# Layer 3 of a four-layer graph network: softmax per block instead of per chunk, and block ends placed by columns

## The chip, the cores and the metric

The kernel runs on one core of a Trainium2 chip. A core has TensorE (PE, matrix products), VectorE (DVE, elementwise work and reductions), ScalarE (ACT, functions such as Exp and Tanh), GpSimd (POOL) and SyncE (SP); every engine works through its own queue in order. Transfers are carried out by 16 DMA engines; a transfer with an index per row ("indirect") is issued from POOL. The metric is the device time of one launch in microseconds, as the median of several runs.

## The reference

3125 nodes with 256 features, 53125 edges sorted by their target. Four layers follow each other; each normalizes x, computes something over the edges and adds it to x. Only layer 3 is changed, a graph attention followed by one gated step:

```
xp = h @ W.T;  a_src = xp @ att_src;  a_dst = xp @ att_dst
src, dst = edges and one loop from each node to itself
e = leaky_relu(a_src[src] + a_dst[dst], 0.2)
alpha = softmax of e over the edges of each target
agg = sum over the edges of a target of alpha * xp[src]
hb = tanh(agg + bias);  i, g, o = hb @ W_ih.T, split (f is not needed)
x = x + sigmoid(o) * tanh(sigmoid(i) * tanh(g))
```

## The kernel before

The nodes are sorted by their number of edges and cut into 25 blocks of 128, one node in each partition. Block b has SLOTS[b] columns: 36 for the first, 24 for the second, and down to 9 for the last, 439 in all. Column q holds the q-th edge of each of the block's nodes, or an empty slot that a penalty `pen` keeps out of the softmax. Before layer 3's edges begin, a table of rows is written to DRAM, one row of 514 numbers for each node: xp (256), a_src, a_dst, and x itself (256).

For each block, one indirect gather ("own", line 1252 by way of line 154) fetches the nodes' own rows, and one gather for every column fetches the first 258 numbers of the source rows into `xg` (also line 154). So there are 439 gathers of columns and 25 of own rows on POOL.

The columns of a block are handled in chunks of at most eight, 66 chunks in all. After a chunk's gathers, VectorE forms the scores z (line 1312), applies the leaky slope (1314) and the penalty (1315), takes the chunk's maximum (1317) and the running maximum (1318), and the difference to the old one (1320). ScalarE takes Exp of the difference (1321) and of the scores (1325). VectorE then sums the denominator (1328, 1330 or 1332), rescales the weighted sum so far (1335), and adds every column times its weight (1338). That is a running softmax. The node's own loop is the start of the sum: its score is the first maximum (1295, 1298), and the own row is the first sum.

The end of a block, `ended`, is a generator in four parts: division and bias and Tanh (1258 to 1262); two transposes and the products with W_ih in four matmuls (1268, 1270); Sigmoid, Tanh and the products (1273 to 1279); and the scatter of the finished rows to the output (line 158). One part is taken per chunk, after that chunk's gathers are written down: so the four parts of a block's end are spread over the first four chunks that follow it.

Three things set the order of the work. Gathers and scatters keep the order in which the program writes them, by explicit links (`queued`, line 139): a gather stands behind every earlier gather and scatter, a scatter behind the last gather. On the other engines a planner lays the instructions in the queue: it prefers what the program writes first, but fills gaps with later work that it takes to be ready. And buffers: `xg` has 6 tiles of 8 columns, `own` 4 tiles, `z3`, `sc3` and `ex` two each.

Of the kernel before, what the change touches and what calls it, by code (L numbers as in the profile page):

```python
# [9 lines left out]
F32 = mybir.dt.float32  # L10
I32 = mybir.dt.int32
BF = mybir.dt.bfloat16
AF = mybir.ActivationFunctionType
ALU = mybir.AluOpType
AX = mybir.AxisListType
# [3 lines left out]
P = 128  # L19
N = 3125  # L20
NB = 25
NP = NB * P
# [3 lines left out]
D = 256  # L26
# [15 lines left out]
SLOTS = (36, 24, 23, 22, 21, 20, 20, 19, 19, 18, 18, 17, 17, 17, 16, 16, 15, 15, 14, 14, 13, 13, 12, 11, 9)  # L42
HALF = tuple((s + 1) // 2 for s in SLOTS)
SM = 36
# [9 lines left out]
XPR = 514  # L54


def flat(ap, n):

    return bass.AP(tensor=ap.tensor, offset=ap.offset, ap=[[n, 1], [1, n]])
# [104 lines left out]
def rows(b):  # L164
    return LAST if b == NB - 1 else P
# [338 lines left out]
def by_slots(ctx, tc, a, out, a_d, nodes_d, ss, t):  # L504
    nc = tc.nc

    def dram(name, shape):
        return nc.dram_tensor(name, shape, F32, kind="Internal").ap()
# [7 lines left out]
    xp_d = dram("s_l3_rows", [NP, XPR])  # L516

    const = ctx.enter_context(tc.tile_pool(name="s_const", bufs=1))
    k = Kit(tc, const)
    Kit.last[:] = [None, None]  # L520
    ident, pcol, jrow = k.ident, k.pcol, k.jrow
    nid_i, nid3_i, deg, has, src_t, pen = t.nid_i, t.nid3_i, t.deg, t.has, t.st[:, :, :, 0], t.pen
# [38 lines left out]
    with tc.tile_pool(name="s_e0", bufs=2) as wk, tc.tile_pool(name="s_e0w", bufs=1) as w, \  # L561
# [42 lines left out]
        for to, of in ((bq, wq), (bkv, wkv)):  # L604
            m = of.shape[2]
            pm = ps.tile([P, 512], F32, name="pm")
            for q in range(2):
                nc.tensor.matmul(pm[:, 0:m], qc[:, q:q + 1].to_broadcast([P, P]), of[:, q, :],
                                 start=(q == 0), stop=(q == 1))
# [129 lines left out]
        def step(n):  # L739

            for _ in range(n):
                if work and next(work[0], work) is work:
                    work.pop(0)
            for t in list(late):
                t[0] -= 1
                if t[0] <= 0:
                    late.remove(t)
                    t[1]()
# [22 lines left out]
        for b in range(NB):  # L771
            S = HALF[b]
            at_, m = ahead
            acc = wk.tile([P, 2, 512], F32, name="acc")
            for s in range(S):
                messages(b, s, stat, m, acc)
                if s == 1 and before is not None:
                    end(b - 1, before)
                if s == S // 2 and b + 1 < NB:
                    ahead = begin(b + 1)  # L780
                if s % 4 == 3 and s + 1 < S:
                    stat = turned(b, at_, s + 1)
                elif s + 1 == S and b + 1 < NB:
                    stat = turned(b + 1, ahead[0], 0)
                if b:
                    scatter_src(1)
                step(1)
            before = acc
        end(NB - 1, before)
        while work or late:  # L790
            step(1)
# [14 lines left out]
    with tc.tile_pool(name="s_e1", bufs=2) as wk, tc.tile_pool(name="s_e1w", bufs=1) as w, \  # L806
# [142 lines left out]
        soon, calm, late1 = [], [], []  # L949
# [14 lines left out]
        for b in range(NB):  # L964
# [4 lines left out]
            sc = wk.tile([P, SM, 4], F32, name="sc")  # L969
            kvs = []  # L970
            for s0 in range(0, SLOTS[b], U):
                s1 = min(s0 + U, SLOTS[b])
# [20 lines left out]
    src3 = apool.tile([P, NB, SM], I32, name="src3")  # L993
    nc.vector.tensor_scalar(src3, src_t, float(XPR), None, op0=ALU.mult)

    wit = apool.tile([P, 2, 768], F32, name="wit")
# [5 lines left out]
    with tc.tile_pool(name="s_e2", bufs=2) as wk, tc.tile_pool(name="s_e2w", bufs=1) as w, \  # L1002
# [8 lines left out]
        for o, (of, cc) in enumerate([("L3_gnn_W_ih", c) for c in (0, 1, 6, 7, 4, 5)] + [("L3_gnn_W", c) for c in (0, 1)]):  # L1011
# [5 lines left out]
            to = wit[:, :, o * P:(o + 1) * P] if o < 6 else wt[:, :, (o - 6) * P:(o - 5) * P]  # L1017
            nc.scalar.copy(to, pt[:, 0:2, :])
        for i, of in enumerate(("L3_gnn_att_src", "L3_gnn_att_dst")):
            at_ = w.tile([P, D], F32, name="at3", bufs=2)  # L1020
            nc.sync.dma_start(at_, bass.AP(tensor=a[of].tensor, offset=a[of].offset, ap=[[0, P], [1, D]]))
            for q in range(2):
                scr = w.tile([P, D], F32, name="scr", bufs=2)
                nc.vector.scalar_tensor_tensor(scr, wt[:, q, 0:D], 1.0, at_, op0=ALU.mult, op1=ALU.mult,
                                               accum_out=wt[:, q, 256 + i:257 + i])
# [121 lines left out]
        soon = []  # L1147
# [98 lines left out]
    with tc.tile_pool(name="s_e3", bufs=2) as wk, tc.tile_pool(name="s_e3w", bufs=1) as w, \  # L1246
            tc.tile_pool(name="s_e3p", bufs=2, space=PSUM) as ps:
        bi = k.load_row(w, a["L3_gnn_bias"], "bi3")

        def owned(b):  # L1250
            own = wk.tile([P, XPR], F32, name="own", bufs=4)
            k.gather(own, flat(xp_d, NP * XPR), nid3_i[:, b:b + 1], axis=1)
            return own

        def ended(b, acc, den, own):

            rd = wk.tile([P, 1], F32, name="rd")
            nc.vector.reciprocal(rd, den)
            y = wk.tile([P, D], F32, name="y")
            nc.vector.scalar_tensor_tensor(y, acc, rd, bi, op0=ALU.mult, op1=ALU.add)  # L1260
            hb = wk.tile([P, D], F32, name="hb")
            nc.scalar.activation(hb, y, AF.Tanh)  # L1262
            yield
            ht = k.transposed(wk, ps, hb, "ht")
            pio = ps.tile([P, 512], F32, name="pio")
            pg = ps.tile([P, D], F32, name="pg")
            for q in range(2):
                nc.tensor.matmul(pio, ht[:, q, :], wit[:, q, 0:512], start=(q == 0), stop=(q == 1))
            for q in range(2):
                nc.tensor.matmul(pg, ht[:, q, :], wit[:, q, 512:768], start=(q == 0), stop=(q == 1))  # L1270
            yield
            io = wk.tile([P, 512], F32, name="io")
            nc.scalar.activation(io, pio, AF.Sigmoid)
            gg = wk.tile([P, D], F32, name="gg", bufs=3)
            nc.scalar.activation(gg, pg, AF.Tanh)
            nc.vector.tensor_mul(gg, gg, io[:, 0:D])
            nc.scalar.activation(gg, gg, AF.Tanh)
            nc.vector.tensor_mul(gg, gg, io[:, D:512])  # L1278
            nc.vector.tensor_add(gg, gg, own[:, 258:XPR])  # L1279
            yield  # L1280
            n = rows(b)
            k.scatter(out, nid_i[:n, b:b + 1], gg[:n], "out")

        soon = []

        def step():
            for g in list(soon):
                if next(g, soon) is soon:
                    soon.remove(g)

        own = owned(0)
        for b in range(NB):
            C = SLOTS[b]
            z1 = wk.tile([P, 1], F32, name="z1")
            nc.vector.tensor_add(z1, own[:, 256:257], own[:, 257:258])

            mx = wk.tile([P, 1], F32, name="mx", bufs=3)
            nc.vector.scalar_tensor_tensor(mx, z1, 0.2, z1, op0=ALU.mult, op1=ALU.max)
            den = None
            acc = own[:, 0:D]  # L1300
            nch = -(-C // 8)
            cuts = [C * i // nch for i in range(nch + 1)]
            for s0, s1 in zip(cuts, cuts[1:]):
                n = s1 - s0
                xg = wk.tile([P, 8, 258], F32, name="xg", bufs=6)
                for q in range(n):
                    k.gather(xg[:, q, :], flat(xp_d, NP * XPR), src3[:, b, s0 + q:s0 + q + 1], axis=1)
                if s1 == C and b + 1 < NB:
                    following = owned(b + 1)
                step()  # L1310
                z = wk.tile([P, 8], F32, name="z3")
                nc.vector.tensor_scalar(z[:, 0:n], xg[:, 0:n, 256], own[:, 257:258], None, op0=ALU.add)  # L1312
                sc = wk.tile([P, 8], F32, name="sc3")
                nc.vector.scalar_tensor_tensor(sc[:, 0:n], z[:, 0:n], 0.2, z[:, 0:n], op0=ALU.mult, op1=ALU.max)  # L1314
                nc.vector.tensor_add(sc[:, 0:n], sc[:, 0:n], pen[:, b, s0:s1])  # L1315
                new = wk.tile([P, 1], F32, name="mx", bufs=3)
                nc.vector.tensor_reduce(new, sc[:, 0:n], AX.X, ALU.max)  # L1317
                nc.vector.tensor_tensor(new, new, mx, ALU.max)
                co = wk.tile([P, 1], F32, name="co")
                nc.vector.tensor_sub(co, mx, new)  # L1320
                nc.scalar.activation(co, co, AF.Exp)
                neg = wk.tile([P, 1], F32, name="neg")
                nc.vector.tensor_scalar(neg, new, -1.0, None, op0=ALU.mult)
                ex = wk.tile([P, 8], F32, name="ex")
                nc.scalar.activation(ex[:, 0:n], sc[:, 0:n], AF.Exp, bias=neg)
                mx = new
                dn = wk.tile([P, 1], F32, name="dn", bufs=3)
                nc.vector.tensor_reduce(dn, ex[:, 0:n], AX.X, ALU.add)
                if den is None:
                    nc.vector.tensor_add(dn, dn, co)  # L1330
                else:
                    nc.vector.scalar_tensor_tensor(dn, den, co, dn, op0=ALU.mult, op1=ALU.add)  # L1332
                den = dn
                to = wk.tile([P, D], F32, name="acc3", bufs=3)
                nc.vector.tensor_scalar(to, acc, co, None, op0=ALU.mult)  # L1335
                acc = to
                for q in range(n):
                    nc.vector.scalar_tensor_tensor(acc, xg[:, q, 0:D], ex[:, q:q + 1], acc, op0=ALU.mult, op1=ALU.add)  # L1338
            soon.append(ended(b, acc, den, own))
            own = following  # L1340
        while soon:
            step()


@with_exitstack
# [890 lines left out]
```

## Time and profile before

| | us |
|---|---|
| median of 3 runs | 4103.96 (4100.12 to 4108.84) |
| the profiled execution's own time | 4300.66 |
| its span | 4298.9 |
| layer 3's edges, from the first own gather to the end of the span | 3545.9 to 4298.9 |

| engine | busy us of the span | share |
|---|---|---|
| PE | 2442.9 | 57% |
| DVE | 2433.4 | 57% |
| ACT | 1116.2 | 26% |
| POOL | 2570.3 | 60% |

The page tells busy time, the costliest groups of instructions, and a chain of work that ended last. A group's line has the line of the code, the engine, the operation, what is written and read, the count, busy time and the mean of one in ns, and after the second bar the idle time of the engine just ahead of these instructions and what ended it. Line 154 is the helper that issues every gather and line 158 the one for every scatter, so these are told apart by the tiles' names: `xg` and `own` for layer 3's gathers, `out_dram` for its scatters. A POOL line shows the time in which the transfer is issued, not the transfer itself. "issue" stands where an engine was idle and waited for nothing that the profile shows; "remote" is an unknown source.

### The profile page before, as it was taken

How to read it: one execution, taken by the hardware profiler on the slowest of the kernel's cores; microseconds unless marked ns; L12 is line 12 of the kernel's file. 1: busy time of each engine (PE TensorE's matmuls, PEld its weight loads, DVE VectorE, ACT ScalarE, POOL GpSimd, SP SyncE). 2: the span in 40 equal slices, each digit the busy share in tenths (PEclk: the TensorE clock that was granted, in tenths of full speed). 3: DMA queues.
4: the chain of work that ended last, by engine and by line, in shares of the span. 5: the costliest groups of instructions: out<-in, count | busy, mean ns of one | idle time of the engine just before them, and what ended most of it. 6: DMA issues, size and time to landing. Idle time of an engine off the chain costs nothing. (4 is left out here: it accounts for less than half of the span.)

```text
span 4298.9 us, 32540 instructions
## 1 busy us (share of the span) xinstructions
PE 2442.9 (57%) x9174; PEld 1508.4 (35%) x9174; DVE 2433.4 (57%) x5099; ACT 1116.2 (26%) x2361; POOL 2570.3 (60%) x2497
## 2 busy tenths in 40 slices
PE   5646766676777743446455466488888860111222
PEld 3213332333333323334344344266566640000011
DVE  5556464546464424556556567378888863444444
ACT  1111121211121112111122222256666640112122
POOL 3547656565655606767767764356666616666665
PEclk9878887888988875667666677689999985555555
DMA  5355454454454425545555554556556533333332
GB/s 198 115 179 148 133 138 136 133 139 131 133 142 123 113 71 143 157 134 148 158 148 156 152 161 150 167 160 191 190 185 193 183 105 90 91 92 94 94 96 76
DMA packets 295539, 595.89 MB, mean 139 GB/s; under 512 B 113201, under 2 KB 154208, under 8 KB 295350
## 3 DMA queue, kind: packets, MB, share of 16 engines
q0 software_dynamic: 163616, 472.86, 37.8%
q1 hardware_dynamic: 131212, 119.79, 9.7%
q8 instruction: 76, 1.25, 0.1%
q10 hardware_dynamic: 522, 1.06, 0.1%
q14 instruction: 113, 0.93, 0.1%
HBM read 510.85 MB, written 82.21 MB: 138 GB/s over the span
## 5 line engine op out<-in xcount | busy, mean ns | idle before, releaser
L154 POOL DMA_INDIRECT kv<-s_l_rows,dst x440 | 435.2, 989 | 318.7 <-PE pg L1136 97.7
L158 POOL DMA_INDIRECT s_src_records<-rec,row x425 | 538.5, 1267 | 129.6 <-issue 128.3
L154 POOL DMA_INDIRECT kv<-s_l_kv,st x439 | 479.8, 1093 | 187.0 <-issue 121.5
L154 POOL DMA_INDIRECT gt<-s_l_src,srcb x452 | 435.1, 963 | 232.0 <-issue 124.0
L654 PE MATMUL ph<-wm,st 128*128 128x512 f32 x904 | 481.0, 661 | 146.6 <-DVE acc L659 69.7
L154 POOL DMA_INDIRECT xg<-s_l_rows,src x439 | 431.6, 983 | 133.8 <-issue 133.8
L655 DVE TENSOR_TENSOR ph<-gt,ph 128x1024 f32<-128x1024 f32 x226 | 277.2, 1227 | 353.9 <-remote 126.9
L843 PE MATMUL pk<-rel,toh 64*128 64x64 f32 x878 | 182.6, 372 | 372.4 <-DVE mk L845 184.9
L134 PE MATMUL pt<-ident,hb 128*128 128x128 f32 x50 | 17.0, 442 | 593.3 <-ACT hb L1262 501.8
L845 DVE TENSOR_TENSOR mk<-kv,pk 128x1024 f32<-128x1024 f32 (+3 forms) x119 | 135.1, 1135 | 374.7 <-DMA kv<-s_l_kv,st 331.4
L654 PEld LDWEIGHTS ph<-wm,st 128*128 128x128 f32 x904 | 174.6, 207 | 388.9 <-issue 320.9
L843 PEld LDWEIGHTS pk<-rel,toh 64*128 64x128 f32 x878 | 165.0, 278 | 404.1 <-issue 355.8
L884 PE MATMUL acc<-kv,ident 128*128 128x256 f32 x878 | 246.1, 448 | 78.6 <-DVE kv L880 53.4
L838 ACT ACTIVATE toh<-tb,negp 64x512 f32<-64x512 f32 (+3 forms) x119 | 81.6, 687 | 681.8 <-PE pk L843 387.2
L1136 PE MATMUL pg<-kv,oh 128*128 128x256 f32 x880 | 256.5, 418 | 3.7 <-DVE kv L1133 3.4
L1338 DVE SCALAR_TENSOR_TENSOR acc<-xg,ex,acc 128x256 f32<-128x256 f32 x439 | 209.6, 483 | 73.9 <-remote 27.6
L659 DVE SCALAR_TENSOR_TENSOR acc<-ph,acc 128x1024 f32<-128x1024 f32 x201 | 245.5, 1221 | 4.3
L884 PEld LDWEIGHTS acc<-kv,ident 128*128 128x128 f32 x878 | 199.0, 230 | 120.0 <-DVE kv L880 57.9
L1097 DVE TENSOR_TENSOR mk<-kv,pk 128x512 f32<-128x512 f32 x220 | 149.8, 681 | 122.7 <-PE pk L1091 43.4
L134 PEld LDWEIGHTS pt<-ident,hb 128*128 128x128 f32 x50 | 7.2, 201 | 604.4 <-ACT hb L1262 510.2
L1091 PE MATMUL pk<-we,eat 64*128 64x256 f32 x880 | 170.6, 461 | 35.3 <-DVE mk L1097 18.1
L1136 PEld LDWEIGHTS pg<-kv,oh 128*128 128x128 f32 x880 | 158.3, 200 | 55.7 <-issue 22.1
(375 smaller groups left out, 5286.2 us busy)
## 6 DMA issues: line engine op xcount, KB each, us to landing
s_src_records<-sfill SPq DMA_DIRECT2D x40, 363.0 KB
srec<-s_src_records SPq DMA_DIRECT2D x24, 594.0 KB
rec<-in_edge_attr_dram SPq DMA_DIRECT2D x25, 531.2 KB
tb<-s_slot_types SPq DMA_DIRECT2D x101, 128.0 KB
gt<-s_l_src,srcb POOLq DMA_INDIRECT x452
kv<-s_l_rows,dst POOLq DMA_INDIRECT x440
kv<-s_l_kv,st POOLq DMA_INDIRECT x439
xg<-s_l_rows,src POOLq DMA_INDIRECT x439
```

The costliest lines, as they stand in the source:

```text
L154: self.queued(lambda: self.nc.gpsimd.indirect_dma_start(out=to, out_offset=None, in_=table, in_offset=bass.IndirectOffsetOnAxis(ap=index, ...
L158: st = self.queued(lambda: self.nc.gpsimd.indirect_dma_start(out=table, out_offset=bass.IndirectOffsetOnAxis(ap=index, axis=0), in_=rows, ...
L654: nc.tensor.matmul(ph[:, h, :], stat[h][:, s % 4, :], m[h], start=True, stop=True)
L655: nc.vector.tensor_add(ph, gt, ph)
L659: nc.vector.scalar_tensor_tensor(acc, ph, 0.0, acc, op0=ALU.max, op1=ALU.add)
L843: nc.tensor.matmul(pk[:, q, :], toh[:, q, :], rel, start=True, stop=True)
L845: nc.vector.tensor_tensor(mk[:, 0:n].rearrange("p s (h d) -> p s h d", h=4), kv[:, 0:n, 0:D].rearrange("p s (h d) -> p s h d", h=4), pk[:, ...
L884: nc.tensor.matmul(acc, ident, v[:, q, :], start=(s0 + q == 0), stop=(s0 + q == C - 1))
L1091: nc.tensor.matmul(pk[:, i, :], eat[i * 64:(i + 1) * 64, q, :], we[i * 64:(i + 1) * 64, :], start=True, stop=True)
L1097: nc.vector.tensor_add(mk, o.kv[j // 2][:, :, 0:D], pk)
L1136: nc.tensor.matmul(pg, oh[:, j % T6 + i, :], v[:, i, :], start=(j + i == 0), stop=(j + i == n - 1))
L1338: nc.vector.scalar_tensor_tensor(acc, xg[:, q, 0:D], ex[:, q:q + 1], acc, op0=ALU.mult, op1=ALU.add)
```

## The change

Layer 3's edge part is written anew, with the same gathers and scatters.

Each block has one softmax over all its columns. Scores are formed for four columns at a time (`score`, three columns after the last of the four was issued) into one tile `sc3` of 36 columns per block. `block` then takes leaky slope, penalty, own score, maximum and exponentials once for the whole block; the denominator comes out of the Exp instruction itself (`accum_out`). The weighted sum starts from the own row, and takes two columns at each later column of the next block.

A block's work is a generator that yields the number of columns to wait until its next part: `tick` is called after every column's gather and counts them down. The block begins 4 columns after its last gather, the sum 2 later; then follow division and Tanh, after 2 the transposes, after 2 the products (g first, then i and o), after 5 the activations, after 3 the first product and Tanh, after 2 the last product and addition, after 3 the scatter. The next block's own row is gathered ahead of the block's last column but one's tick, where before it came after the last column. `xg` has 20 tiles of four columns, `own` 6 tiles, `sc3` 4.

```diff
-            own = wk.tile([P, XPR], F32, name="own", bufs=4)
+            own = wk.tile([P, XPR], F32, name="own", bufs=6)
...
+        def block(b, own, sc, xgs):
+            C = SLOTS[b]
+            s = sc[:, 0:C]
+            nc.vector.scalar_tensor_tensor(s, s, 0.2, s, op0=ALU.mult, op1=ALU.max)
+            nc.vector.tensor_add(s, s, pen[:, b, 0:C])
+            one = wk.tile([P, 4], F32, name="one", bufs=3)
+            z1, mx, co, den = (one[:, i:i + 1] for i in range(4))
+            nc.vector.tensor_add(z1, own[:, 256:257], own[:, 257:258])
+            nc.vector.scalar_tensor_tensor(z1, z1, 0.2, z1, op0=ALU.mult, op1=ALU.max)
+            nc.vector.tensor_reduce(mx, s, AX.X, ALU.max)
+            nc.vector.tensor_scalar(mx, mx, z1, -1.0, op0=ALU.max, op1=ALU.mult)
+            nc.scalar.activation(co, z1, AF.Exp, bias=mx)
+            nc.scalar.activation(s, s, AF.Exp, bias=mx, accum_out=den)
+            yield 2
+            nc.vector.tensor_add(den, den, co)
+            nc.vector.reciprocal(den, den)
+            acc = wk.tile([P, D], F32, name="acc3", bufs=3)
+            nc.vector.tensor_scalar(acc, own[:, 0:D], co, None, op0=ALU.mult)
+            for q in range(C):
+                nc.vector.scalar_tensor_tensor(acc, xgs[q // U3][:, q % U3, 0:D], s[:, q:q + 1], acc,
+                                               op0=ALU.mult, op1=ALU.add)
+                if q % 2:
+                    yield 1
             y = wk.tile([P, D], F32, name="y")
-            nc.vector.scalar_tensor_tensor(y, acc, rd, bi, op0=ALU.mult, op1=ALU.add)
+            nc.vector.scalar_tensor_tensor(y, acc, den, bi, op0=ALU.mult, op1=ALU.add)
...
-            yield
+            yield 2
             ht = k.transposed(wk, ps, hb, "ht")
+            yield 2
...
+        def tick():
+            for e in list(todo):
+                e[0] -= 1
+                if e[0] <= 0:
+                    e[0] = next(e[1], None)
+                    if e[0] is None:
+                        todo.remove(e)
+
+        def score(sc, own, xg, q0, q1):
+            nc.vector.tensor_scalar(sc[:, q0:q1], xg[:, 0:q1 - q0, 256], own[:, 257:258], None, op0=ALU.add)
+            yield 1
...
-            for s0, s1 in zip(cuts, cuts[1:]):
...
+            sc = wk.tile([P, SM], F32, name="sc3", bufs=4)
+            xgs = []
+            for q in range(C):
+                if q % U3 == 0:
+                    xgs.append(wk.tile([P, U3, 258], F32, name="xg", bufs=20))
+                k.gather(xgs[-1][:, q % U3, :], flat(xp_d, NP * XPR), src3[:, b, q:q + 1], axis=1)
+                if q % U3 == U3 - 1 or q == C - 1:
+                    todo.append([3, score(sc, own, xgs[-1], q - q % U3, q + 1)])
+                if q == C - 2 and b + 1 < NB:
+                    following = owned(b + 1)
+                tick()
+            todo.append([4, block(b, own, sc, xgs)])
             own = following
-        while soon:
-            step()
+        while todo:
+            tick()
```

## The prediction

> **What bounds the kernel now.** I read the page's costliest groups first. The change touches layer 3 alone, which runs from 3545.9 us to the end of the span at 4298.9: 753 of 4298.9 us.
>
> ```profile
> L154 POOL DMA_INDIRECT xg<-s_l_rows,src x439 | 431.6, 983 | 133.8 <-issue 133.8
> L1338 DVE SCALAR_TENSOR_TENSOR acc<-xg,ex,acc 128x256 f32<-128x256 f32 x439 | 209.6, 483 | 73.9 <-remote 27.6
> ```
>
> POOL needs 983 ns for each of 439 gathers, with 0.305 us of "issue" before each; DVE, the next engine, has 483 ns a column. Second, busy time by stage (columns: length, then PE, PEld, DVE, ACT and POOL busy, clock, DMA share, GB/s):
>
> ```profile
> 3640.00:3656.00 16.00, 4.89 (x10) 2.24 (x10) 14.44 (x61) 6.14 (x14) 0.06 (x1) 0.71 0.00 0
> ...
> 3765.00:4042.00 277.00, 50.08 (x93) 23.35 (x94) 126.01 (x508) 53.04 (x120) 187.43 (x191) 0.56 0.35 95
> ```
>
> In the long stage 191 POOL issues with their gaps are 187.4 + 191 x 0.305 = 245.7 of 277 us, while DVE is busy 45% and the DMA engines 35%. In the 16 us above it POOL stands still and DVE catches up, 61 instructions. Third, POOL's waits from 3545 to 4270 us (total, times, longest):
>
> ```profile
> POOL out_dram L158 <- DVE dn L1332: 72.0, 11, 22.0
> POOL out_dram L158 <- DVE gg L1279: 17.1, 3, 7.5
> POOL out_dram L158 <- DVE dn L1330: 12.8, 2, 8.4
> ```
>
> No gather waits for a buffer; the scatters wait, and gathers queue behind them. Fourth, the order of time around one scatter, POOL and then DVE:
>
> ```profile
> 3688.45 0.95 POOL L154 DMA_INDIRECT xg<-s_l_rows,src  x1 [0.31 <-issue]
> 3692.84 1.12 POOL L158 DMA_INDIRECT out_dram<-gg,nid_i  x1 [3.44 <-DVE dn L1332]
> ```
> ```profile
> 3691.20 0.23 DVE L1312 TENSOR_SCALAR z<-xg,own 128x7 f32<-128x7 f32 x1 [4.20 <-DMA xg<-s_l_rows,src]
> 3691.34 0.42 DVE L1278 TENSOR_TENSOR gg<-gg,io 128x256 f32<-128x256 f32 x1
> ...
> 3692.14 0.42 DVE L1279 TENSOR_TENSOR gg<-gg,own 128x256 f32<-128x256 f32 x1
> ```
>
> The scatter's rows (L1279) stand on DVE behind the score z of the newest chunk. That chunk lands 2.75 us after its last gather starts, so the scatter waits 3.44 us. Note that z was put ahead of L1278, which the program writes earlier: DVE's order is the planner's.
>
> POOL's account closes. From 3545.9 to 4274.4 are 728.5 us: 487 issues (439 + 25 own + 23 scatters) at 1.254 us start to start, 610.7; scatter waits 107.7 less 23 x 0.305, 100.7; longer issues (983 against 949 ns, scatters 1.07 us) 17. Behind it stands a tail of 24.5 us.
>
> Two oddities matter.
>
> ```profile
> 3613.28 0.48 DVE L1338 SCALAR_TENSOR_TENSOR acc<-xg,ex,acc 128x256 f32<-128x256 f32 x1 [1.17 <-DVE mx L1298]
> 3614.67 0.16 DVE L1318 TENSOR_TENSOR mx<-mx 128x1 f32<-128x1 f32 x1 [0.91 <-DVE acc L1338]
> 3617.47 0.48 DVE L1338 SCALAR_TENSOR_TENSOR acc<-xg,ex,acc 128x256 f32<-128x256 f32 x1 [2.64 <-remote]
> ```
> ```profile
> 3658.39 2.85 DVE L1338 SCALAR_TENSOR_TENSOR acc<-xg,ex,acc 128x256 f32<-128x256 f32 x7
> 3658.68 1.00 POOL L154 DMA_INDIRECT xg<-s_l_rows,src  x1 [0.30 <-issue]
> 3659.99 2.86 POOL L154 DMA_INDIRECT xg<-s_l_rows,src  x1 [0.30 <-issue]
> ```
>
> First, in six stretches DVE starts late by 0.9 to 2.6 us for data of its own that is long done: 6 to 9 starts in 10 us instead of 14 to 20. The six scatters behind them waited 22.0, 12.5, 7.5, 4.8, 4.8 and 8.4 us; the eleven other waits have a mean of 4.2. Second, seven weighted sums back to back stretched a gather to 2.86 us.
>
> **What the Trainium skill says.** "SBUF — State Buffer", Who interferes with whom: a DVE instruction with two SBUF inputs contends with a GpSimd instruction that reads SBUF, and who starts first holds the port. The trace agrees in direction (2.86 us), but usually mildly: 34 ns a gather on average. "VectorE: DVE Perf Modes", The TRN2 errata: every SBUF instruction pays a fixed latency, and cycles grow with the free size; agreed, 128x1 takes 145 to 157 ns. "Perfetto Trace Analysis", DMA Instruction — SWDGE: the reported end is the end of descriptor generation, not of the data; agreed, a 0.95 us gather lands 2.75 us after its start. So I count POOL start to start.
>
> **The change, part by part.** *One softmax a block.* Per chunk (66) go two score steps, two maxima, subtraction, negation and reduction of the denominator; their rows, with z, are 257+160+162+155+157+156+145+152 ns, 88.7 us. The denominators (12.7 us) and 41 of 66 rescalings (15.2) go too. Added are 119 scores of four columns at 0.257, 30.6 us, and per block six operations on 36 columns or fewer (estimate: 150 to 160 ns plus up to 30 ns, from the errata's one cycle an element): 25 x 0.85 = 21. DVE falls from 390 to about 326 us and from 1274 to 883 instructions. None of it is on POOL's path: worth nothing by itself. On ACT 132 exponentials become 50; the accumulating form is not in the trace, and I bound it by no extra and one more small instruction (0.2 us x 25), off the path. Table loads stay near two a block (1.28 us each), since a block still goes from Exp to Sigmoid once.
>
> *Gathers, own rows and scatters* keep their number: 489 issues. No transfer is added, no other queue crossed. Twenty tiles of four columns are 80 columns of room instead of 48; a block, its successor's half and six columns fill at most 60, so a gather should still not wait.
>
> *Block ends at counted distances.* The sum starts 6 columns after the block's last gather and takes half its columns; the scatter comes 24 + C/2 columns after, 3 columns (3.8 us) behind its last addition. The chain between is far shorter than the distance: for 20 columns 34 x 1.25 = 43 us against 20 x 0.52 (sum with a small operation in each gap, from the 16 us catch-up) + about 8 (two transposes, 3.6 + 1.3 us of matmuls, table load, four activations). So the data wait of the scatter goes; what can remain is DVE's order. If the planner again puts the newest complete score ahead of the last products, the wait is 2.75 - 1.25 + 1.1 (score and two products) = 2.6 us when a four has just ended, 1.4, 0.1 and 0 at one to three columns later: mean 1.0. Behind a score that waits for its landing stand, in DVE's one queue, all sums, products and y; ACT's activations and, last, POOL's scatter wait for those. Bounds: 0 (program order), 4.2 (as now). I take three in four of the mean, 0.75 x 23 = 17 us.
>
> *What comes back.* All sums now run while POOL works, none in its pauses; L1338 and gathers overlap more, so I let the 15 us of stretching grow to 25 (bounds 15 and 70, the latter gathers at 1.1 us). In the tail the last block sums nine columns after its softmax instead of five (4 x 0.48) and about six sums of the block before are still ahead (2.9): +5 us (bounds 0 and 10).
>
> Sum against the profiled execution: -100.7 + 17 + 10 + 5 = -69, 4298.9 to about 4230. The profiled run took 4300.66, the median is 4103.96, 197 us less, and I don't know where. If late DVE starts are lighter without the profiler, the excess of the six waits, 60 - 6 x 4.2 = 35 us, isn't there to be won; I take half, 18. Forecast: -51, **4053 us**.
>
> **Rivals.** *A, full gain:* no scatter wait remains and the late starts are real: -100 + 5 = 4009. For it: POOL's account closes with nothing else. *B, half:* late starts last longer, since each stretch now ended only when POOL paused; at 0.7 starts a us against 883 in 630 us needed, 1.4, DVE falls back and scatters wait at half today's rate: about -18, 4086. *C, no change:* sums beside every gather stretch each by 0.12 us, 489 x 0.12 = 59, and the gain is eaten: 4104. *D, slower:* the planner pulls scores of all gathered fours ahead of the sums (today one chunk, as z bufs allow; now four score tiles and twenty xg). Then each scatter waits for the landing, 2.75, and up to nine sums left behind it, 4.3: 7 us x 23 = 161, against 100.7 now: +60 +15, 4179. It decides from 3.7 us a scatter ((100.7 - 15) / 23). For it: z before L1278 above. Against: a four's score needs few operations, and DVE has 48% free.
>
> **Numbers.** A measurement of this kernel tells about 0.2%, 8 us. Forecast 0.55 (its own range 4028 to 4080), A 0.13, B 0.12, C 0.06, D 0.14. Faster 0.80, same 0.06, slower 0.14. The range drops D's far side and A's edge: 4010 to 4112.
>
> **What would show it.** Right: scatter waits on POOL of about 17 us in all, from the first own gather to the last gather near 655 us, gathers still "issue"-bound at about 1.25 us, DVE 883 instructions. Wrong: gathers waiting for xg's release, mean gather above 1.05 us, scatter waits of 4 us or more with a score or a row of sums just ahead of the block's last addition, or a tail above 35 us.

## The result

The changed kernel takes 4113.97 us in the median of 16 runs (4106.11 to 4125.0), the kernel before 4104.23 us in 16 runs (4097.13 to 4115.26). The ratio is 1.0027, with a 95% interval of 1.0016 to 1.0037: slower by about 10 us, where 51 us less were forecast. The time lies just above the stated range.

The profiled execution of the changed kernel has a span of 4111.6 us, close to its timed runs. That of the kernel before, on which the prediction rests, was 197 us above its own. So I read the after against a second profiled execution of the kernel before, which was made for it as the first experiment (span 4103.3 us).

Three groups of layer 3 of the after, as on its page:

```profile
L154 POOL DMA_INDIRECT xg<-s_l_rows,src x439 | 430.9, 982 | 133.9 <-issue 133.9
L1321 DVE TENSOR_SCALAR sc<-xg,own 128x4 f32<-128x4 f32 (+3 forms) x119 | 30.5, 256 | 321.5 <-DMA xg<-s_l_rows,src 314.3
L1278 DVE SCALAR_TENSOR_TENSOR acc<-xg,sc,acc 128x256 f32<-128x256 f32 x439 | 211.0, 484 | 7.9
```

and the scores of the kernel before in its second profile:

```profile
L1312 DVE TENSOR_SCALAR z<-xg,own 128x7 f32<-128x7 f32 (+4 forms) x66 | 17.1, 258 | 334.4 <-DMA xg<-s_l_rows,src 329.7
```

A gather costs what it did (982 against 983 ns), the "issue" ahead of it too. VectorE (DVE) spends 314.3 us idle in front of scores, waiting for gathers to land. That is not new: in the second profile of the before it is 329.7 us. What differs is the work that stands behind such a score. Busy time in two stages of the after, from the first own gather to the last column's gather, and the tail (columns as in the prediction):

```profile
3392.00:4079.00 687.00, 129.01 (x228) 62.99 (x229) 280.37 (x846) 106.70 (x220) 476.75 (x486) 0.55 0.36 98
4079.00:4111.60 32.60, 12.67 (x23) 5.66 (x21) 13.39 (x37) 9.58 (x18) 3.85 (x4) 0.66 0.07 19
```

and of the kernel before in its second profile:

```profile
3395.00:4077.00 682.00, 131.36 (x232) 61.23 (x232) 309.78 (x1242) 130.79 (x290) 478.08 (x486) 0.56 0.36 99
4077.00:4103.30 26.30, 8.17 (x18) 3.95 (x18) 9.31 (x32) 7.00 (x15) 4.23 (x4) 0.69 0.10 26
```

DVE does about 400 instructions fewer, and nothing comes of it: the stream of gathers is 5 us longer and the tail 6 to 7 us, together about the 10 us of the timed runs. POOL's waits in the stream of the after:

```profile
POOL out_dram L158 <- DVE gg L1305: 65.8, 12, 9.8
```

and in that of the before, second profile:

```profile
POOL out_dram L158 <- DVE dn L1332: 47.3, 11, 5.1
POOL out_dram L158 <- DVE dn L1330: 8.9, 2, 4.5
POOL out_dram L158 <- DVE dn L1328: 4.0, 1, 4.0
```

Less the usual 0.305 us ahead of each issue, the 22 scatters in the stream wait 62.2 us in the after and 55.9 us in the before. The DVE instruction after the arrow is the one whose signal the profile saw last; the scatter's rows are finished by L1279 before and L1305 after, close beside it in the queue. The waits that the change was expected to take away are there again, in another pattern: for the first blocks of the after, the usual 0.3 included, 9.4, 0.3, 9.8, 0.3, 8.6, 0.3 and 7.4 us. One of them in order of time, POOL first, then DVE:

```profile
3560.78 1.00 POOL L154 DMA_INDIRECT xg<-s_l_rows,src  x1 [0.30 <-issue]
3562.09 0.95 POOL L154 DMA_INDIRECT xg<-s_l_rows,src  x1 [0.30 <-issue]
3572.88 0.99 POOL L158 DMA_INDIRECT out_dram<-gg,nid_i  x1 [9.84 <-DVE gg L1305]
```
```profile
3564.98 0.23 DVE L1321 TENSOR_SCALAR sc<-xg,own 128x4 f32<-128x4 f32 x1 [2.97 <-DMA xg<-s_l_rows,src]
3565.12 5.17 DVE L1278 SCALAR_TENSOR_TENSOR acc<-xg,sc,acc 128x256 f32<-128x256 f32 x10
3570.20 0.42 DVE L1301 TENSOR_TENSOR gg<-gg,io 128x256 f32<-128x256 f32 x1
3570.54 1.00 DVE L1278 SCALAR_TENSOR_TENSOR acc<-xg,sc,acc 128x256 f32<-128x256 f32 x2
3571.45 0.42 DVE L1304 TENSOR_TENSOR gg<-gg,io 128x256 f32<-128x256 f32 x1
3571.78 0.48 DVE L1278 SCALAR_TENSOR_TENSOR acc<-xg,sc,acc 128x256 f32<-128x256 f32 x1
3572.18 0.42 DVE L1305 TENSOR_TENSOR gg<-gg,own 128x256 f32<-128x256 f32 x1
```

DVE stands at a score until 3564.98, 2.9 us after the last gather was started. Ten sums (L1278) whose columns landed long before come behind that score in its queue, then the products L1301, L1304 and L1305 with three more sums among them. In the program L1305 comes three columns ahead of this scatter, and the score of the columns gathered right up to it comes after it; in the queue L1305 lies behind that score. This is the mechanism of the prediction's rival D, with a mean wait of 62.2 / 22 = 2.8 us instead of D's 7.

### The profile page after: what moved, and what is told of

It is laid out like the page before. It is cut to its first block, busy times and chain, and to the rows that moved or that the text cites. A ratio compares the mean times of both kernels' runs of the same rounds, so it can differ in the third digit from the quotient of the medians.

```text
span 4111.6 us, 32048 instructions
## 1 busy us (share of the span) xinstructions
PE 2403.7 (58%) x9174; PEld 1495.2 (36%) x9174; DVE 2396.2 (58%) x4708; ACT 1093.7 (27%) x2294; POOL 2579.6 (63%) x2497
## 3 DMA queue, kind: packets, MB, share of 16 engines
q8 instruction: 76, 1.25, 0.1%
## 5 line engine op out<-in xcount | busy, mean ns | idle before, releaser
L154 POOL DMA_INDIRECT kv<-s_l_rows,dst x440 | 458.2, 1041 | 206.9 <-issue 71.3
L654 PE MATMUL ph<-wm,st 128*128 128x512 f32 x904 | 465.6, 642 | 166.2 <-DVE acc L659 129.6
L1321 DVE TENSOR_SCALAR sc<-xg,own 128x4 f32<-128x4 f32 (+3 forms) x119 | 30.5, 256 | 321.5 <-DMA xg<-s_l_rows,src 314.3
L1278 DVE SCALAR_TENSOR_TENSOR acc<-xg,sc,acc 128x256 f32<-128x256 f32 x439 | 211.0, 484 | 7.9
L158 POOL DMA_INDIRECT s_l_kv<-kv,nid_i x25 | 24.8, 993 | 240.7 <-DVE kv L731 229.9
```

Of the source, the lines that this page charges most:

```text
L154: self.queued(lambda: self.nc.gpsimd.indirect_dma_start(out=to, out_offset=None, in_=table, in_offset=bass.IndirectOffsetOnAxis(ap=index, ...
L158: st = self.queued(lambda: self.nc.gpsimd.indirect_dma_start(out=table, out_offset=bass.IndirectOffsetOnAxis(ap=index, axis=0), in_=rows, ...
L654: nc.tensor.matmul(ph[:, h, :], stat[h][:, s % 4, :], m[h], start=True, stop=True)
L1278: nc.vector.scalar_tensor_tensor(acc, xgs[q // U3][:, q % U3, 0:D], s[:, q:q + 1], acc, op0=ALU.mult, op1=ALU.add)
```

## Experiments

Times are against the kernel before, run beside each on the same chip; its medians there were 4100.7, 4105.91 and 4101.6 us.

**The kernel before, profiled again.** No edit.

> The kernel before, profiled once more, nothing changed. Theory (the late DVE starts belonged to that one execution): no stretch in which DVE starts late for data long done; scatter waits on POOL about 65 us in the stream instead of 100.7, layer 3 about 710 us instead of 753. Rival (late starts are in every execution): waits again near 100 us, layer 3 near 750.

Measured 4105.15 us; layer 3's edges take 708.0 us (753.0 in the first profile), with 55.9 us of scatter waits in the stream and not one late start of DVE. (A late start is here one that comes over 0.4 us after the previous instruction and waits for no semaphore but DVE's own; the first profile has 87.) So the theory held. Nor is there a late start in any of the nine other profiles of this study. So the late starts and the three longest waits belonged to that execution. What caused them, and the 150 us that this execution lost ahead of layer 3, stays open.

**DVE in the program's order.** The after, and each DVE instruction of layer 3's edges tied behind the one written before it:

```diff
+        # V forwards to nc.vector, with every call inside:
...
+                        with tc.issue_after(InOrder.last):
+                            st = getattr(nc.vector, name)(*p, **kw)
+                    InOrder.last = st.ins
...
-            nc.vector.tensor_scalar(sc[:, q0:q1], ...)
+            V.tensor_scalar(sc[:, q0:q1], ...)
```

> The kernel after, with every DVE instruction of layer 3's edges tied behind the one that the program writes before it, so that the planner can't reorder them. Theory (the scatters wait because the planner lets two blocks' sums alternate and puts a block's last products behind the next block's sums): scatter waits fall from 66 to under 15 us, time about 4114 - 55 = 4059. Rival (the data themselves are late, or DVE is too slow beside the gathers): waits stay above 50 us, time 4105 to 4115. Second rival (program order makes DVE stop at each dependence): waits move to gathers that wait for xg, time above 4120.

Measured 4046.05 us, ratio 0.986 (0.984 to 0.988), 13 us below the forecast 4059. POOL's waits at scatters in the stream (L1261 is the line of the tie, so all DVE instructions have it):

```profile
POOL out_dram L158 <- issue: 3.7, 12, 0.3
POOL out_dram L158 <- DVE acc L1261: 2.1, 7, 0.3
POOL out_dram L158 <- DVE sc L1261: 0.6, 2, 0.3
POOL out_dram L158 <- DVE y L1261: 0.3, 1, 0.3
```

All 22 are at the 0.3 us of an issue: nothing is left. The stream falls from 686.2 to 623.7 us (first own gather to the start of the last gather), with the same gathers, operations, buffers and distances. The data are not late and DVE is not too slow; the order alone makes the wait. Which part of the order does it, this run does not tell.

**Own rows scattered, in the after and in the before.** The scatter waits for a row that landed long ago:

```diff
-            k.scatter(out, nid_i[:n, b:b + 1], gg[:n], "out")
+            k.scatter(out, nid_i[:n, b:b + 1], own[:n, 258:XPR], "out")
```

> The kernel after, but each scatter writes the block's own rows (landed long before) instead of the finished rows: the output lacks layer 3's part, all work is still done. It prices the scatter waits. Theory (waits are the whole loss on POOL): stream shorter by 66 us and the tail's waits gone too, time 4035 to 4050. Rival (the stall moves to gathers waiting for xg or to the DMA engines): time above 4080.

> The kernel before with the same edit: own rows are scattered, the output lacks layer 3's part. Theory (both kernels have the same floor on POOL and the before had about as much scatter wait as the after): time 4035 to 4050, like the after's twin within 10 us. Rival (the before's waits were the 100 us of its first profile): about 4005. Rival (with only six xg tiles of eight the gathers then wait for xg): above 4060.

Measured 4073.27 us for the after (0.993, 0.9909 to 0.9951) and 4059.35 us for the before (0.989, 0.9868 to 0.9913); both expectations missed, above their 4050, and the two lie 14 us apart, not within 10. All waits in the stream are gone in both, but the mean gather grew to 1024 and 1009 ns: 439 x (1024 - 982) = 18 us of the after's gain went into the gathers. From the timeline of the after's twin:

```profile
3473.84 7.59 DVE L1278 SCALAR_TENSOR_TENSOR acc<-xg,sc,acc 128x256 f32<-128x256 f32 x19
3474.61 0.95 POOL L154 DMA_INDIRECT xg<-s_l_rows,src  x1 [0.30 <-issue]
3475.86 1.24 POOL L154 DMA_INDIRECT xg<-s_l_rows,src  x1 [0.30 <-issue]
3477.40 5.25 POOL L154 DMA_INDIRECT xg<-s_l_rows,src  x1 [0.30 <-issue]
```

Nineteen sums, 0.40 us apart, hold one gather for 5.25 us. Sums that run while POOL stands at a scatter can stretch no gather; with the wait taken away and the planner's order kept, such rows run beside gathers.

**One block's sums at a time.** In the after's queue the sums of two blocks take turns in places. One tie a block forbids this:

```diff
-            nc.vector.tensor_scalar(acc, own[:, 0:D], co, None, op0=ALU.mult)
...
+                with tc.issue_after(ended[0]):
+                    nc.vector.tensor_scalar(acc, own[:, 0:D], co, None, op0=ALU.mult)
...
-            nc.vector.scalar_tensor_tensor(y, acc, den, bi, op0=ALU.mult, op1=ALU.add)
+            ended[0] = nc.vector.scalar_tensor_tensor(y, acc, den, bi, op0=ALU.mult, op1=ALU.add).ins
```

> The kernel after, with a single tie a block: the weighted sum of a block may start only behind the previous block's division y; everything else stays the planner's. Theory (two blocks' sums take turns, so that both end late, together): scatter waits fall from 62 to under 12 us, time 4050 to 4065. Rival (it is the scores pulled ahead that do it, sums in turn or not): waits stay above 30 us, time above 4075.

Measured 4104.53 us in 20 runs, ratio 1.0004 (0.9993 to 1.0016). My theory fell: turns are not the cause of the waits. The stream still has 55.4 us of them, now on 17 of the 22 scatters (12.4, 0.5, 6.7, 0.3, 6.1, 2.6, 4.2, 2.7 us at first):

```profile
POOL out_dram L158 <- DVE gg L1310: 60.6, 17, 12.4
```

The turns may well account for the small loss against the before, which is gone here: the waits are 6.8 us less than in the after, and the mean gather is 971 ns instead of 982, 5 us in all. One of the waits on its timeline:

```profile
3620.83 0.95 POOL L154 DMA_INDIRECT xg<-s_l_rows,src  x1 [0.30 <-issue]
3622.54 0.23 DVE L1326 TENSOR_SCALAR sc<-xg,own 128x4 f32<-128x4 f32 x1 [3.04 <-DMA xg<-s_l_rows,src]
3622.68 2.56 DVE L1283 SCALAR_TENSOR_TENSOR acc<-xg,sc,acc 128x256 f32<-128x256 f32 x5
...
3627.14 0.42 DVE L1310 TENSOR_TENSOR gg<-gg,own 128x256 f32<-128x256 f32 x1
...
3627.84 0.98 POOL L158 DMA_INDIRECT out_dram<-gg,nid_i  x1 [6.06 <-DVE gg L1310]
```

Again a score that waits for the newest columns, and behind it sums and products. The turns did make the pairs of one long and one short wait.

**Scores tied.** The complement: in the after, each of the 119 scores is tied behind the DVE instruction written just before it, all else is the planner's.

```diff
-            nc.vector.tensor_scalar(sc[:, q0:q1], xg[:, 0:q1 - q0, 256], own[:, 257:258], None, op0=ALU.add)
...
+                # V notes the last DVE instruction written
+                with tc.issue_after(Noted.last):
+                    V.tensor_scalar(sc[:, q0:q1], xg[:, 0:q1 - q0, 256], own[:, 257:258], None, op0=ALU.add)
```

> The kernel after, with only the 119 scores tied, each behind the VectorE instruction that the program writes just before it; sums, products and softmax steps stay the planner's. It is the complement of the run with one sum at a time. Theory (scores pulled ahead of sums make DVE stop for gathers and leave a row of sums for the time after the last landing): scatter waits fall from 62 to under 10 us, time 4045 to 4060, like the full program order. Rival (two causes share the wait, turns of sums and pulled scores, and each alone keeps most of it): waits 30 us or more, time above 4070.

Measured 4045.05 us, ratio 0.9862 (0.9842 to 0.9883), as with everything tied. In the stream 3.4 us of waits are left; the longest:

```profile
POOL out_dram L158 <- DVE gg L1257: 4.3, 3, 1.9
```

With the program order and one block's sums at a time, this settles it: the scores that the planner pulls ahead of sums and products make the waits.

**The scatter later, in the after.** `yield 13` for `yield 3` ahead of the scatter, and `gg` with 5 buffers.

> The kernel after, with the scatter 13 columns behind the last addition instead of 3 (gg in 5 buffers): 10 columns are 12.5 us, more than the longest wait of 9.8. Theory (order fixed by the planner, a wait of bounded length): waits under 10 us, but rows of sums now run beside gathers and stretch single ones to several us, as with own rows scattered (mean 1023 ns): time 4060 to 4075. Rival (the planner uses the room and puts the last products later still): waits above 40 us, time above 4095.

Measured 4074.43 us, ratio 0.9925 (0.9908 to 0.9942). The time is as expected; waits in the stream are 19.9 us, more than expected (10.4 us at the first block), and the mean gather is 994 ns, one of them 5.24 us. Ten columns of distance take the ratio of the after from 1.0027 to 0.9925, about six tenths of what order takes it.

**The before with its scatter a chunk later, and the before in program order.**

```diff
             nc.vector.tensor_add(gg, gg, own[:, 258:XPR])
             yield
+            yield
             n = rows(b)
             k.scatter(out, nid_i[:n, b:b + 1], gg[:n], "out")
```

In the first, `gg` also has 4 buffers. The second is the tie of the program order, put around the before's DVE instructions.

> The kernel before, running softmax and all, with the scatter one chunk (about 7 columns, 8.8 us) later and gg in 4 buffers: the smallest edit of the before that gives the scatter distance. Theory (the distance is what was worth, the one softmax is not): waits fall from 56 to under 8 us, some gathers stretched: time 4050 to 4065. Rival (DVE's 1274 instructions are too many beside running gathers): waits above 30 us, time above 4080.

> The kernel before with all its DVE instructions of layer 3's edges in the program's order. Theory (the planner's order makes the waits in the before as well, by putting the newest chunk's score ahead of the last products): waits under 8 us, time 4045 to 4060, within 10 us of the after in program order, so that the one softmax alone is worth under 10 us. Rival (a running softmax in strict order stops at each Exp, so DVE falls behind): waits or gathers waiting for xg above 30 us, time above 4080.

Measured 4051.58 us (0.9874, 0.9854 to 0.9895), with 4.0 us of waits in the stream, and 4046.96 us (0.9848, 0.9831 to 0.9864), with none:

```profile
POOL out_dram L158 <- issue: 5.5, 18, 0.3
POOL out_dram L158 <- DVE acc L1259: 0.9, 3, 0.3
POOL out_dram L158 <- DVE y L1259: 0.3, 1, 0.3
```

The before, with 1274 DVE instructions and a running softmax, ends in program order where the after with 883 does (0.9848 and 0.986, intervals that overlap). The one softmax is worth nothing here. Three versions beat the kernel before by 1.4 to 1.5%: each softmax in program order, and the after with its scores tied. One `yield` in the before wins nearly as much (0.9874).

## Why the prediction was wrong

*What bounds the kernel* was right: POOL's issues, 1.25 us each, and the waits at its scatters. With the waits gone by order, both softmaxes run 55 to 59 us below the kernel before.

*The size of the gain to be had* was too large. The 100.7 us of waits came from an execution with late DVE starts; an undisturbed one has 55.9. I took half of the excess, 18 us; it should have been all 45. The oddity was seen and named, and the eleven waits with a mean of 4.2 us already told most of it: 100.7 - 35 is 65.7.

*What remains of the waits* is the step that failed. I took 0.75 us a scatter, from a model in which at most the score and two products stand behind the newest landing. Measured are 2.8 us a scatter and up to 9.8, in all 62.2 us where 17 were forecast: 45 of the 61 us by which the forecast missed. The term that the model lacks is sums. Counted in the after's trace, 8 to 13 of them stand between the last score that DVE stopped at and L1305, in each of the seven longest waits; in the second profile of the before at most one stands there, in any of its 14 waits. That is also the sign of being wrong that the prediction named: waits of 4 us or more with a row of sums just ahead of the last addition. The warning lay in the profile that I showed, z ahead of L1278, and in rival D's nine sums, to which I gave 0.14.

That the after's larger buffers let the planner pull further, as D supposed, the traces do not show. Against the queues in program order, a score stands up to 18 instructions too early in the after (4 in the mean) and up to 16 in the before (8 in the mean). Why the planner puts scores there is not on record either; that it takes gathers to be quicker than they are is a guess. What is seen is that DVE stops at each such score until the columns land, and that the sums left over come after it while POOL waits.

*Rival D's turning point*, 3.7 us a scatter, used the disturbed 100.7. With 55.9 and a tail 7 us longer it is (55.9 - 6.8) / 22 = 2.2 us; the measured 2.8 lies above it, which agrees with the small loss.

*Gathers stretched by sums:* +10 us forecast, none measured; it was 18 us where own rows are scattered and POOL does not stand at scatters. *The tail:* +5 forecast, +6.8 measured (26.5 to 33.3 us from the start of the last gather). *DVE's work:* 390 to 326 us and 883 instructions forecast, 392.6 to 330.5 us and 883 measured (the new operations of a block are five, not six; 0.85 us a block is the price of five); that it is worth nothing by itself was right, as the runs in program order show. *Gathers waiting for xg:* none, as forecast. The accumulating Exp is two instructions, 0.30 and 0.19 us on ACT, off the path: within its bounds.

The sum of what was measured: -55.9 + 62.2 of waits, -1 of scatters (1.07 to 1.03 us), +6.8 of tail, together +12 us against 719.5 - 708.0 = 11.5 in the two profiles and 9.7 in the medians.

## What to carry to other kernels

Where a planner orders an engine's queue, a distance in the program is no distance in the queue: look in the trace for an instruction that waits for a transfer ahead of work that is long ready, and count what stands behind it that somebody else waits for. A tie between each such waiting instruction and the work written before it was worth 1.4% here, and nearly a third fewer instructions on that engine nothing. And before a wait is costed, the profiled execution has to match the timed runs: one that is 5% above them needs a second profile.

## What the runs showed of the hardware

Gathers are stretched beside sums that follow each other closely. In program order, where each sum needs the one before, eight of them take 4.14 us, 0.52 us apart, and no gather is longer than 1.21 us:

```profile
3463.76 4.14 DVE L1261 SCALAR_TENSOR_TENSOR acc<-xg,sc,acc 128x256 f32<-128x256 f32 x8
3464.58 1.00 POOL L154 DMA_INDIRECT xg<-s_l_rows,src  x1 [0.30 <-issue]
3465.89 0.95 POOL L154 DMA_INDIRECT xg<-s_l_rows,src  x1 [0.30 <-issue]
```

Sums of two blocks in turn follow each other 0.40 us apart, and then a gather can stand until the row ends, 5.25 us in the run with own rows above. With one block's sums at a time no sums are that close, and again no gather is longer than 1.22 us. Counted over all eleven traces, with the sums from 0.3 us ahead of a gather's start to 0.95 us after it: of 1060 gathers beside sums 0.48 us or more apart, one took over 1.3 us (1.43); of 159 beside sums 0.40 us apart, 30 did; of the 3608 beside no two sums in a row, 20 did, at most 1.74.

"SBUF — State Buffer" of the Trainium skill, Who interferes with whom, says that a DVE instruction with two SBUF inputs contends with a GpSimd instruction that reads SBUF. The runs agree in direction for a closed row; whether a gather counts as such an instruction, no run here shows. Dependent sums lie 0.12 us further apart; that this is what lets a gather through is inferred from the spacing and wasn't tried alone.
